# Fetching the second expert layer's first three weight tiles during the last batch's attention

## The chip, the cores and the metric

The kernel runs on one core of one Trainium2 chip. The metric is device time in microseconds (us): the median of three runs. A core has TensorE (PE, matmuls), VectorE (DVE), ScalarE (ACT), GpSimd (POOL) and SyncE (SP, which here only issues transfers). Transfers (DMAs) are issued from the queues of SP, ACT and POOL.

## The reference

Two layers over `x` (4 batches of 512 tokens, 256 wide), with a context of 1601 rows for each batch. Each layer is a cross-attention and then a mixture of eight experts.

```python
x = x + _L0_xattn_ref(ctx_1024, _layernorm(x), ...)      # 8 heads of 128
x = x + _L0_ffn_ref(_layernorm(x), ...)                  # top 2 of 8 experts, with a capacity
x = x + _L1_xattn_ref(ctx_1024, _layernorm(x), ...)      # 8 heads of 32
x = x + _L1_ffn_ref(_layernorm(x), ...)                  # weights of the 2 best of 8 experts

def _L1_ffn_ref(x, W1, b1, W2, b2, Wr, br):
    logits = xf @ Wr + br
    topv, _ = lax.top_k(logits, TOPK)
    masked = jnp.where(logits >= topv[:, TOPK - 1:TOPK], logits, -jnp.inf)
    weights = jax.nn.softmax(masked, axis=-1)
    h = jax.nn.gelu(jnp.einsum('td,edh->eth', xf, W1) + b1[:, None, :], approximate=False)
    expert_out = jnp.einsum('eth,ehd->etd', h, W2) + b2[:, None, :]
    out = jnp.einsum('etd,te->td', expert_out, weights)
```

All numbers are float32. In the last layer the kernel computes an expert only for the tokens that chose it, in tiles of 256 tokens.

## The kernel before

**Four stages.** The first attention (to about 1640 us), the first expert layer (to about 1936), the second attention (to about 2650) and the second expert layer (to the end). The change touches the last two.

**Memory.** Tiles are taken from pools, and pools lie in the on-chip memory one above the other, in the order in which they are opened; a pool that is closed leaves its place to pools opened later. `gat` (eight tiles of 256 columns), `kv1` (keys `kT0`, `kT1` and values `v1` of the second attention, two buffers of each) and `w1p` (`wT`, the attention's three weight matrices, and `cT`, the context turned round, one buffer) are opened before the first expert layer. `kv1` and `w1p` hang on a stack of their own, `kvst`. The second attention opens its own pools above them (`c_one`, `c_two`, `c_six`) and closes them at its end; then `kvst.close()` (L1381) gives up `kv1` and `w1p` too, and the last stage opens `d_one` to `d_spare` from there up. `d_four` has four buffers `w` for an expert's weights: 4104 columns, which are the first layer's matrix (`WB1`, 2048 columns), the second layer's (2048) and the bias (8). `d_spare` has one more.

**The second attention.** 16 units: batch, half of the heads (`o`), half of the tokens (`f`), each of 13 steps, one for each 128 rows of the context. A step computes scores (`ps_w`, L1188), their exponential (ACT, `pT`), its sum over rows (`sum`, on DVE, every third on POOL) and weighs the values (`ps_o`, L1219). `put(step, f)` places other work between: keys and values of the batch after next or so (`keys_values`, in the middle batches), the queries of the next batch, loads of `keyed` and `asked` (SP), the expert outputs of the first expert layer (`collect`, POOL), and `route2`, the last layer's router, for the batch before (from step 10 of a batch, every second step). `route2` normalizes the tokens into `pay`, chooses experts, gives every token a place, writes the corrected `x` to the output (SP, L514) and sends `pay` row by row to its place in two lists in memory, `rows_a` (the first 256 tokens of each expert from batches 0 to 2) and `rows_b` (the others), by indirect DMAs of POOL (L521). Sends to one list wait for each other. Within this stage the order of PE, DVE, ACT and POOL is that of the program (`in_order`). SP's order, and everything in the last stage, is placed by the framework.

At step 4 of the last batch `load_first_weights` (L1279) fetches the first layer's matrix of expert 0, 2048 columns, into the eight tiles of `gat`.

**The second expert layer.** 21 tiles: 8 of `rows_a`, one for each expert (`first_tile`, fetched by SP), then 13 of `rows_b` (`further_tile`, fetched by POOL, indirect, at places that `table` computes). For each tile: the tokens (`rows`, three buffers) are turned by four PE transposes and one DVE copy (`turned`: `tp2`, `xT2`, L1439 and L1440); `told` copies where each token goes (`to`, L1401, five buffers) and its weight (`share`, L1429); `hidden` is the first layer (`ps_h`, L1451, with Gelu on ACT, L1459, that reads the bias from the weights); `results` is the second layer (`ps_y`, L1470), DVE scales it (`y`, L1497) and POOL adds it to the output (L1483). The loop of L1623 runs, for tile i: first layer of i, two steps of the last batch's routing (`rest`), fetch of tile i+2, tokens of tile i+1 turned, second layer of tile i-1. In `first_tile(0)` the second layer's matrix and the bias come as `w2_first` (the profile calls it `w_first`). What is left over after 21 tiles (`beyond`, `ties`) is done only if the counts ask for it; the counts are computed in `table` and read by `values_load` (L1641).

Of the kernel before, what the change touches and what calls it, by code (L numbers as in the profile page):

```python
# [8 lines left out]
F32 = mybir.dt.float32  # L9
I32 = mybir.dt.int32  # L10
# [6 lines left out]
P = 128  # L17
B, S, D = 4, 512, 256
M = 1601
# [30 lines left out]
T = B * S  # L50
# [8 lines left out]
WB2 = WB1 + FC * D  # L59
WIDE = WB2 + FC  # L60


# [5 lines left out]
def xattn_ffn_twice(ctx: ExitStack, tc: tile.TileContext, a: dict, out: bass.AP):  # L68
# [855 lines left out]

# [124 lines left out]
    with ExitStack() as st:  # L1049
# [229 lines left out]
        def load_first_weights():  # L1279


            for i in range(0, WB1, D):
# [97 lines left out]

    kvst.close()  # L1381


    with ExitStack() as st:
        one = st.enter_context(tc.tile_pool(name="d_one", bufs=1))
        two = st.enter_context(tc.tile_pool(name="d_two", bufs=2))
        three = st.enter_context(tc.tile_pool(name="d_three", bufs=3))
        four = st.enter_context(tc.tile_pool(name="d_four", bufs=4))
        five = st.enter_context(tc.tile_pool(name="d_five", bufs=5))
# [6 lines left out]
        def told(rows, share_of):  # L1396
# [6 lines left out]
            return rows, to, share  # L1403

        def columns(t):
            return lambda i, n: t[:, i : i + n]

        def first_tile(e):

            rows = []  # L1410
            for r in range(GR):
                got = three.tile([P, PAY], F32, tag=f"rows{r}", name=f"rows{r}")
                nc.sync.dma_start(got, rows_a[e * G + r * P : e * G + (r + 1) * P, :])
                rows.append(got)
            if e == 0:
                w2 = one.tile([P, WIDE - WB1], F32, name="w2_first")
                nc.sync.dma_start(w2, a["wall"][:P, WB1:])
                w = lambda i, n: (
                    first_weights[i // D][:, i % D : i % D + n]
                    if i < WB1  # L1420
                    else w2[:, i - WB1 : i - WB1 + n]
                )
            else:
                t = four.tile([P, WIDE], F32, tag="w", name="w_e")
                nc.sync.dma_start(t, a["wall"][e * P : (e + 1) * P, :])
# [77 lines left out]
        def table():  # L1503
# [64 lines left out]
            state.update(mine=mine, w_idx=w_idx, x_idx=x_idx, counts=counts_i)  # L1568

        state = {}  # L1570

        def further_tile(i, three=three, four=four):

            rows = []
            for r in range(GR):
# [11 lines left out]
                rows.append(got)  # L1587
            t = four.tile([P, WIDE], F32, tag="w", name="w_e")
            nc.gpsimd.indirect_dma_start(
# [23 lines left out]
        more = [lambda e=e: first_tile(e) for e in range(2, E)]  # L1613
        more += [lambda i=i: further_tile(i) for i in range(SURE)]
        more.append(lambda: further_tile(SURE, spare, spare))

# [24 lines left out]
        n_tiles = nc.values_load(state["counts"][0:1, 0:1], min_val=0, max_val=NG)  # L1641
        ties = nc.values_load(state["counts"][0:1, 1:2], min_val=0, max_val=E * T)

        def beyond(i, fetched=None):
            with tc.If(n_tiles > i):
                w, xT, to, share = ready(*(fetched or further_tile(i)))
                results(w, to, share, hidden(w, xT))
                if i + 1 < NG:
                    beyond(i + 1)

        beyond(SURE, fetched.pop())

        with tc.If(ties > 0):
            for b in range(B):
                for t0 in range(0, NT, GR):
# [19 lines left out]
                    for e in range(E):  # L1677
                        t = spare.tile([P, WIDE], F32, tag="w", name="w_t")
                        nc.sync.dma_start(t, a["wall"][e * P : (e + 1) * P, :])
# [82 lines left out]
```

## Time and profile before

| what | value |
|---|---|
| median of 3 runs | 2993.43 us (2989.96 to 2995.0) |
| the profiled execution | 2993.88 us, its span 2992.2 us |
| PE busy | 2778.0 us (93%) |
| DVE, ACT, POOL busy | 1456.4, 933.3, 400.0 us |
| first attention, 0 to 1650 | PE 1569.9 us busy |
| first expert layer, 1650 to 1936 | PE 278.8 of 286 |
| second attention, 1936 to 2651 | PE 617.8 of 715, DMA share 0.12 |
| start of the second expert layer, 2651 to 2729 | PE 62.5 of 78, DMA share 0.54 |
| its rest, 2729 to 2992 | PE 249.1 of 263, DMA share 0.52 |
| fetch of one expert's weights by SP (`w_e`) | 2052 KB, 7 times |

Times in the views are microseconds from the start of the span. A line of a timeline gives start, duration, engine, line of the kernel, operation, output and input with their sizes, how often, and in brackets how long the engine had been idle and what ended it. A buffer's number is left out of its name, so `w_g` is the weights in `gat`, and `ps_h` all buffers of that name. The DMA share is the mean busy share of the 16 DMA engines.

### The profile page before, as it was taken

Reading aid. Unit: us, or ns where it says so; the run is one execution under the profiler, and the core shown is the slowest. Engines: PE = TensorE matmul, PEld = TensorE weight load, DVE = VectorE, ACT = ScalarE, POOL = GpSimd, SP = SyncE. Lnnn points to the kernel's source line nnn. Section 1 sums busy time; section 2 is a strip of 40 time slices with the busy share of each in tenths; the row PEclk is TensorE's granted clock in tenths of the full one; section 3 lists DMA queues with packets and bytes.
Section 4 is the critical chain, followed back from the end, with each engine's and each line's share of the span. In section 5 each row is a group of like instructions: output and inputs, shape, how many; then the busy total and the mean of one; then the engine's idle time right before and its main releaser. Section 6 shows DMA issues by size and latency. Waiting matters only on the chain.

```text
span 2992.2 us, 35534 instructions
## 1 busy us (share of the span) xinstructions
PE 2778.0 (93%) x13426; PEld 1839.3 (61%) x13426; DVE 1456.4 (49%) x2324; ACT 933.3 (31%) x1312; POOL 400.0 (13%) x308
## 2 busy tenths in 40 slices
PE   5699999999999999999997999879989898898998
PEld 2466676667766667666665566634444444466887
DVE  4256447544475444554454200178777768741110
ACT  2133234323343233333331221124434344341221
POOL 1000000100001000000000100022314223333442
PEclk9899999999999999999998899979999999898999
DMA  8743334433344333333334333110101110055552
GB/s 297 236 124 95 98 92 103 117 92 89 95 113 109 90 94 91 99 93 97 95 94 120 117 106 115 47 46 17 28 24 41 29 37 23 11 181 169 185 173 72
DMA packets 165103, 295.95 MB, mean 99 GB/s; under 512 B 43287, under 2 KB 81752, under 8 KB 161848
## 3 DMA queue, kind: packets, MB, share of 16 engines
q1 hardware_dynamic: 124024, 204.45, 24.4%
q0 software_dynamic: 16320, 53.42, 5.9%
q10 hardware_dynamic: 24576, 35.68, 4.6%
q8 instruction: 109, 1.79, 0.3%
q14 instruction: 74, 0.61, 0.1%
HBM read 97.86 MB, written 49.76 MB: 49 GB/s over the span
## 4 chain that ended last, share of the span: by engine, by line
PE 82%; DVE 7%; issue 3%; DMA 3%; ACT 3%; SPq 2%; POOL 1%; POOLq 0%; DVEq 0%; ACTq 0%
PE ps_o L772 15%; PE ps_s L735 15%; PE ps_v L718 7%; PE ps_k L685 7%; PE ps_w L1188 6%; PE ps_y L1470 4%; PE ps_h L1451 4%; PE ps_h L970 4%; PE ps_y L983 4%; DVE tops L1149 2%; PE ps_o L1219 2%; DVE sum L1210 2%; PE ps_p L783 2%; PE ps_v L945 2%; PE ps_q L670 2%
## 5 line engine op out<-in xcount | busy, mean ns | idle before, releaser
L743 DVE TENSOR_REDUCE top<-ps_s 128x1 f32<-128x2113 f32 x128 | 301.8, 2358 | 574.8 <-PE ps_s L735 574.8
L772 PE MATMUL ps_o<-pT,v 128*128 128x256 f32 x2176 | 521.5, 382 | 7.7 <-DVE pT L764 7.7
L735 PE MATMUL ps_s<-kT,qT 128*128 128x512 f32 (+1 forms) x1280 | 488.9, 527 | 26.3 <-ACT attn L749 26.0
L772 PEld LDWEIGHTS ps_o<-pT,v 128*128 128x128 f32 x2176 | 411.4, 191 | 124.8 <-issue 70.3
L735 PEld LDWEIGHTS ps_s<-kT,qT 128*128 128x128 f32 x1280 | 241.8, 191 | 275.7 <-issue 239.9
L749 ACT ACTIVATE attn<-ps_s,top 128x2113 f32<-128x2113 f32 x128 | 259.0, 2024 | 486.5 <-DVE top L743 448.8
L764 DVE STREAM_TRANSPOSE pT<-swapped 128x2176 f32<-128x2176 f32 x128 | 312.4, 2441 | 70.8 <-DMA swapped<-attn 60.3
L1149 DVE TENSOR_REDUCE tops<-ps_s 128x2 f32<-128x1024 f32 (+1 forms) x224 | 237.4, 1104 | 135.2 <-PE ps_s L1138 135.0
L685 PE MATMUL ps_k<-kvin,wkv 128*128 128x512 f32 (+1 forms) x640 | 262.0, 534 | 5.0 <-ACT kT L692 5.0
L1188 PE MATMUL ps_w<-asked,keyed 64*128 64x256 f32 (+1 forms) x1664 | 244.2, 415 | 20.5 <-DVE tops L1149 9.5
L718 PE MATMUL ps_v<-wkv,kvin 128*128 128x256 f32 x1088 | 253.5, 381 | 0.0
L1201 ACT ACTIVATE pT<-ps_w 128x1024 f32<-128x1024 f32 (+1 forms) x176 | 179.5, 1024 | 192.5 <-PE ps_w L1188 190.4
L1188 PEld LDWEIGHTS ps_w<-asked,keyed 64*128 64x128 f32 (+1 forms) x1664 | 147.0, 189 | 143.2 <-ACT pT L1201 60.7
L718 PEld LDWEIGHTS ps_v<-wkv,kvin 128*128 128x128 f32 x1088 | 204.9, 190 | 32.7 <-issue 3.3
L1210 DVE TENSOR_TENSOR sum<-sum,pT 128x1024 f32<-128x1024 f32 (+1 forms) x128 | 181.0, 1414 | 10.7 <-ACT pT L1201 3.9
L692 ACT ACTIVATE kT<-ps_k,bqk 128x512 f32<-128x512 f32 (+1 forms) x160 | 97.3, 621 | 268.7 <-DMA swapped<-attn 129.8
L1210 POOL TENSOR_TENSOR sum<-sum,pT 128x1024 f32<-128x1024 f32 x48 | 124.1, 2585 | 345.7 <-ACT pT L1201 345.5
L685 PEld LDWEIGHTS ps_k<-kvin,wkv 128*128 128x128 f32 x640 | 116.5, 192 | 80.9 <-issue 67.1
L1451 PE MATMUL ps_h<-xT,w_e 128*128 128x256 f32 x640 | 143.9, 383 | 10.2 <-issue 10.2
L1138 PE MATMUL ps_s<-kT,qT 32*128 32x512 f32 (+1 forms) x1024 | 140.5, 577 | 12.5 <-ACT kT L936 6.8
L725 ACT COPY v<-ps_v 128x512 f32<-128x512 f32 x144 | 80.0, 561 | 224.9 <-PE ps_v L718 156.2
L1470 PE MATMUL ps_y<-w_e,hT 128*128 128x256 f32 x640 | 144.4, 385 | 0.0
(261 smaller groups left out, 2615.1 us busy)
## 6 DMA issues: line engine op xcount, KB each, us to landing
swapped<-attn SPq DMA_DIRECT2D x1536, 68.0 KB
swapped<-attn ACTq DMA_DIRECT2D x512, 68.0 KB
rows_b<-empty SPq DMA_DIRECT2D x36, 530.0 KB
w<-in_w_dram SPq DMA_DIRECT2D x16, 1024.0 KB
w_e<-in_wall_dram SPq DMA_DIRECT2D x7, 2052.0 KB
cT<-in_ctxT_dram SPq DMA_DIRECT2D x4, 1601.0 KB
keyed<-kT SPq DMA_DIRECT2D x32, 200.1 KB
ctx_b<-in_ctx_dram SPq DMA_DIRECT2D x4, 1536.0 KB
```

The costliest lines, as they stand in the source:

```text
L685: nc.tensor.matmul(ps[:, :n], lhsT=wkv[:, c, hs], rhs=flat_kvin[c][:, j0 : j0 + n], start=c == 0, stop=c == DC - 1,)
L718: nc.tensor.matmul(ps[:, k, :], lhsT=flat_kvin[c][:, j * P : (j + 1) * P], rhs=wkv[:, c, cols], start=c == 0, stop=c == DC - 1,)
L735: nc.tensor.matmul(flat[:, j0 : j0 + n], lhsT=qT[:, t * P : (t + 1) * P], rhs=kT[:, j0 : j0 + n], start=True, stop=True,)
L743: nc.vector.tensor_reduce(top, flat[:, :L], AX.X, ALU.max, negate=True)
L749: nc.scalar.activation(attn[:, :L], flat[:, :L], AF.Exp, bias=top, accum_out=total)
L764: nc.vector.transpose(pT[:, :, k * P : (k + 1) * P].rearrange("p c (a i) -> p a c i", a=4), swapped.rearrange("p a (c i) -> p a c i", i=32),)
L772: nc.tensor.matmul(ps, lhsT=v[:, j - parts[part][0], (h % 2) * DH0 : (h % 2 + 1) * DH0], rhs=pT[:, j, :], start=j == 0, stop=j == NB - 1,)
L1149: nc.vector.tensor_reduce(tops[u][:, t : t + at // n, 2 * pair : 2 * pair + 2, j0 // 512], of, AX.X, ALU.max,)
L1188: nc.tensor.matmul(ps[:r, s, pair * QH : (pair + 1) * QH], lhsT=keyed[o][64 * s : 64 * s + 64, pair, j * P : j * P + r], rhs=asked[u % 3][ ...
L1210: (nc.gpsimd if k else nc.vector).tensor_tensor(to, to, pT[:r], ALU.add)
L1451: nc.tensor.matmul(ps[:, f, :], lhsT=w(at, P), rhs=xT[:, c, :], start=c == 0, stop=c == DC - 1,)
L1470: nc.tensor.matmul(ps, lhsT=hT[:, f, r * P : (r + 1) * P], rhs=w(WB1 + f * D, D), start=f == 0, stop=f == FC - 1,)
```

## The change

Keys and values of a batch become one tile `kv` (6530 columns, two buffers), context and the attention's weights one tile `cw` (4738 columns). `load_first_weights`, still at step 4 of the last batch, now fetches three tiles' weights whole: expert 0's rest and expert 1's into the next buffer of `kv` (that of batch 2), expert 2's into `cw`. `kvst.close()` is gone, and so are `d_four`, `w2_first` and the spare tile's own weights: `room(k)` gives the weights of tile k two buffers of `kv`, `cw`, or the one buffer of the new pool `d_new`, in turn. The fetches of tiles 3 to 7 are kept behind SP's transfer before them in the program (`keep_in_program_order`: an order in the queue, no wait for its end). The integer copy of the counts is made in iteration 18 of the loop and not in `table`.

```diff
+KV = DC * M + NM * D
...
-    wT = w1p.tile([P, 3, DC, D], F32, name="wT")
+    cw = w1p.tile([P, DC * (M + 3 * D)], F32, name="cw")
+    cT = cw[:, : DC * M].rearrange("p (c m) -> p c m", c=DC)
+    wT = cw[:, DC * M :].rearrange("p (k c o) -> p k c o", k=3, c=DC)
...
-        cT = w1p.tile([P, DC, M], F32, tag="cT", name="cT")
         nc.sync.dma_start(cT, a["ctxT"][b].rearrange("(c p) m -> p c m", p=P))
-        kT = [kv1.tile([P, M], F32, tag=f"kT{o}", name=f"kT{o}") for o in range(DC)]
-        v = kv1.tile([P, NM, D], F32, tag="v1", name="v1")
+        kv = kv1.tile([P, KV], F32, tag="kv", name="kv")
+        kT = [kv[:, o * M : (o + 1) * M] for o in range(DC)]
+        v = kv[:, DC * M :].rearrange("p (j d) -> p j d", d=D)
...
             for i in range(0, WB1, D):
                 g = gat.tile([P, D], F32, tag="g", name="w_g")
                 nc.sync.dma_start(g, a["wall"][:P, i : i + D])
-                first_weights.append(g)
+                gs.append(g)
+            t = kv1.tile([P, KV], F32, tag="kv", name="w_kv")
+            rest = t[:, WIDE:]
+            nc.sync.dma_start(rest[:, : WIDE - WB1], a["wall"][:P, WB1:])
+            nc.sync.dma_start(t[:, :WIDE], a["wall"][P : 2 * P, :])
+            nc.sync.dma_start(cw[:, :WIDE], a["wall"][2 * P : 3 * P, :])
...
-    kvst.close()
...
-        four = st.enter_context(tc.tile_pool(name="d_four", bufs=4))
+        new = st.enter_context(tc.tile_pool(name="d_new", bufs=1))
...
+        def room(k):
+            if k % 4 == 2:
+                return cw[:, :WIDE]
+            if k % 4 == 3:
+                return new.tile([P, WIDE], F32, tag="w", name="w_e")
+            return kv1.tile([P, KV], F32, tag="kv", name="w_e")[:, :WIDE]
...
-            if e == 0:
-                w2 = one.tile([P, WIDE - WB1], F32, name="w2_first")
-                nc.sync.dma_start(w2, a["wall"][:P, WB1:])
...
+            if e < len(first_weights):
+                w = first_weights[e]
             else:
-                t = four.tile([P, WIDE], F32, tag="w", name="w_e")
-                nc.sync.dma_start(t, a["wall"][e * P : (e + 1) * P, :])
+                t = room(e)
+                tc.keep_in_program_order(
+                    nc.sync.dma_start(t, a["wall"][e * P : (e + 1) * P, :])
+                )
...
-            counts_i = one.tile([P, 2], I32, name="counts_i")
-            nc.vector.tensor_copy(counts_i, counts)
...
-        more.append(lambda: further_tile(SURE, spare, spare))
+        more.append(lambda: further_tile(SURE, E + SURE, spare))
...
+            if i == E + SURE - 3:
+                counts_i = one.tile([P, 2], I32, name="counts_i")
+                tc.keep_in_program_order(nc.vector.tensor_copy(counts_i, state["counts"]))
```

More of the change, by code (lines that the diff above doesn't have):

```diff
@@ L60 @@
 WIDE = WB2 + FC
+KV = DC * M + NM * D
+assert KV >= 2 * WIDE - WB1
 def rows_of(i, n, tail):
@@ L1279, in load_first_weights @@
         def load_first_weights():
+            gs = []
             for i in range(0, WB1, D):
@@ L1284, in load_first_weights, with first @@
                 nc.sync.dma_start(g, a["wall"][:P, i : i + D])
-                first_weights.append(g)
+                gs.append(g)
[4 more added lines that the diff above has]
+            nc.sync.dma_start(cw[:, :WIDE], a["wall"][2 * P : 3 * P, :])
+            def first(i, n):
+                return gs[i // D][:, i % D : i % D + n] if i < WB1 else rest[:, i - WB1 : i - WB1 + n]
+            first_weights.append(first)
+            first_weights.append(lambda i, n: t[:, i : i + n])
+            first_weights.append(lambda i, n: cw[:, i : i + n])
         def put(step, *fs):
@@ L1414, in first_tile @@
                 rows.append(got)
[L1415 to L1425 removed]
+            if e < len(first_weights):
+                w = first_weights[e]
+            else:
+                t = room(e)
+                tc.keep_in_program_order(
+                    nc.sync.dma_start(t, a["wall"][e * P : (e + 1) * P, :])
+                )
                 w = columns(t)
@@ L1567, in table, with further_tile @@
                 nc.vector.tensor_copy(x_idx[:, r, :], x_at)
-            state.update(mine=mine, w_idx=w_idx, x_idx=x_idx, counts=counts_i)
+            state.update(mine=mine, w_idx=w_idx, x_idx=x_idx, counts=counts)
         state = {}
-        def further_tile(i, three=three, four=four):
+        def further_tile(i, k, three=three):
             rows = []
@@ L1587, in further_tile @@
                 rows.append(got)
-            t = four.tile([P, WIDE], F32, tag="w", name="w_e")
+            t = room(k)
             nc.gpsimd.indirect_dma_start(
@@ L1613, in xattn_ffn_twice @@
         more = [lambda e=e: first_tile(e) for e in range(2, E)]
-        more += [lambda i=i: further_tile(i) for i in range(SURE)]
-        more.append(lambda: further_tile(SURE, spare, spare))
+        more += [lambda i=i: further_tile(i, E + i) for i in range(SURE)]
+        more.append(lambda: further_tile(SURE, E + SURE, spare))
         def ready(w, rows, share_of):
@@ L1636, in xattn_ffn_twice @@
             last = (w, to, share, hT, T - S if i < E else T)
+            if i == E + SURE - 3:
+                counts_i = one.tile([P, 2], I32, name="counts_i")
+                tc.keep_in_program_order(nc.vector.tensor_copy(counts_i, state["counts"]))
         results(*last)
         assert next(rest, None) is None
-        n_tiles = nc.values_load(state["counts"][0:1, 0:1], min_val=0, max_val=NG)
-        ties = nc.values_load(state["counts"][0:1, 1:2], min_val=0, max_val=E * T)
+        n_tiles = nc.values_load(counts_i[0:1, 0:1], min_val=0, max_val=NG)
+        ties = nc.values_load(counts_i[0:1, 1:2], min_val=0, max_val=E * T)
         def beyond(i, fetched=None):
             with tc.If(n_tiles > i):
-                w, xT, to, share = ready(*(fetched or further_tile(i)))
+                w, xT, to, share = ready(*(fetched or further_tile(i, 2 + i % 2)))
                 results(w, to, share, hidden(w, xT))
@@ L1649, in beyond @@
                     beyond(i + 1)
+        assert (E + SURE) % 4 < 2
         beyond(SURE, fetched.pop())
@@ L1677, in xattn_ffn_twice @@
                     for e in range(E):
-                        t = spare.tile([P, WIDE], F32, tag="w", name="w_t")
+                        t = room(2 + e % 2)
                         nc.sync.dma_start(t, a["wall"][e * P : (e + 1) * P, :])
```

## The prediction

> **What bounds the kernel now.** I read the busy time by stretches first. TensorE (PE) is busy 93% of the span, so only a stretch where it is not can give anything back. The columns are the stretch, its length, then busy time of PE, PE's weight loads, VectorE (DVE), ScalarE (ACT) and GpSimd (POOL), granted clock, DMA share, GB/s.
>
> ```profile
> 2651.00:2729.00 78.00, 62.47 (x287) 52.63 (x288) 24.21 (x129) 17.87 (x38) 17.55 (x15) 0.89 0.54 183
> 2729.00:2992.00 263.00, 249.09 (x1185) 218.70 (x1183) 37.78 (x135) 57.12 (x136) 101.15 (x79) 0.98 0.52 158
> ```
>
> After 2729 the second expert layer runs without gaps, 14.26 us a tile (6.91 first layer, 6.91 second, 0.44 transposes). The change can only matter from the end of attention (2644) to 2729, where tile 4's first layer begins. PE in that stretch:
>
> ```profile
> 2650.91 5.45 PE L1451 MATMUL ps_h<-xT,w_g 128*128 128x256 f32 x24
> 2658.43 1.10 PE L161 MATMUL tp<-ident,pay 128*128 128x128 f32 x6 [2.08 <-DVE pay L392]
> 2659.36 1.89 PE L1451 MATMUL ps_h<-xT,w_g 128*128 128x256 f32 x8
> 2661.09 0.38 PE L161 MATMUL tp<-ident,pay 128*128 128x128 f32 x2
> ...
> 2704.88 8.99 PE L1451 MATMUL ps_h<-xT,w_e 128*128 128x256 f32 x32 [9.52 <-issue]
> ...
> 2719.55 0.61 PE L1510 MATMUL ps_x<-over,ones 128*128 128x16 f32 x2 [3.93 <-DVE xT L1440]
> ```
>
> The gaps are 2.08, 9.52 and 3.93 us. None ends with a weight landing, although three tiles' weights are fetched just here. The two long ones end when DVE turns the tokens (`xT`). DVE says why:
>
> ```profile
> 2656.06 0.15 DVE L1401 CAST to<-rows 128x1 int32<-128x1 f32 x1 [3.15 <-DMA rows_b<-pay,place_b]
> ...
> 2703.85 0.15 DVE L1401 CAST to<-rows 128x1 int32<-128x1 f32 x1 [21.81 <-DMA out_dram<-y,to]
> ...
> 2718.68 0.21 DVE L1401 CAST to<-rows 128x1 int32<-128x1 f32 x2 [12.87 <-DMA out_dram<-y,to]
> ```
>
> `to` has five buffers. The sixth tile's `to` takes tile 0's, so it waits until tile 0's sums have been added to the output. It stands ahead of `xT` of tile 3 in DVE's queue; the seventh's does the same to tile 4. Those additions are issued by POOL:
>
> ```profile
> 2671.48 0.97 POOL L521 DMA_INDIRECT rows_b<-pay,place_b  x1 [17.86 <-PE ps_h L1451]
> 2676.53 0.97 POOL L521 DMA_INDIRECT rows_b<-pay,place_b  x1 [4.09 <-DMA rows_b<-pay,place_b]
> ...
> 2704.26 0.99 POOL L521 DMA_INDIRECT rows_b<-pay,place_b  x1 [7.16 <-DMA rows_b<-pay,place_b]
> 2709.03 0.97 POOL L521 DMA_INDIRECT rows_b<-pay,place_b  x1 [3.78 <-DMA rows_b<-pay,place_b]
> ```
>
> Eight sends of the last batch's rows go one after the other, each waiting for the one before, and the additions to the output sit between and behind them. The chain of waits runs through the same names. So the stretch is bound by this: the router's decision for the last batch (`place_b`, 2670.73), eight sends, four additions (the last issued at 2714.81, landed by 2718.6), `to`, `xT`, and 10.5 us later tile 4 (2729.09).
>
> **The change, part by part.**
>
> *Early fetch.* Three added DMAs on SP's queue (SyncE's), 1028 + 2052 + 2052 KB, some 0.33 us of issue each, and some 13 to 20 us of transfer at the 424 to 259 GB/s of 2655 to 2665. They wait for batch 2's last use of `kv` (a `ps_o` at about 2507) and the last use of `wT` (`ps_q`, 2445 to 2447). Cost nothing: from 2510 to 2550 the DMA share is 0.00 to 0.05. Behind them on SP stand the loads of `asked` for units 14 and 15 (2504 and 2537 now); each is used 13 or more steps of some 2.7 us after its buffer comes free, so 35 us of slack cover even a load that stands behind all 20 us; without that cover a late load would cost up to those 20 us. The merged `kv` tile is freed by the last `ps_o`, which PE has passed before the next keys are evacuated: nothing.
>
> *Removed from the transition:* `w_first` and the first two `w_e`, 5.1 MB. SP now:
>
> ```profile
> 2625.04 2.71 SPq L1413 DMA_DIRECT2D rows<-rows_a  x6
> 2644.13 0.33 SPq L1417 DMA_DIRECT2D w_first<-in_wall_dram  x1
> 2655.33 0.81 SPq L1425 DMA_DIRECT2D w_e<-in_wall_dram  x2
> ```
>
> While `w_first` moved, batch 2's third-last send (2643.45, 1.80 of issue) took until 2649.7; the next two took 2.5 us from issue to landing, and the last landed at 2655.19. With 2.5 minus 0.97, about 1.6, after the issue: 2646.9, then 2 x 2.7, gives 2652.3. **Gain 2.9 us** at that point, call it R.
>
> *What waits for R.* The part of the diff that is easy to pass over is the removed `kvst.close()`. The pools of the last stage lie one above the other. Before, the small ones (`d_one` with `w2_first`, `d_two`, `d_three`: 11.7 + 44.9 + 6.5 = 63 KB a partition by their tile shapes) took the 71 KB that keys, values, context and `wT` left. That is why `rows` could be fetched at 2625 and tile 0 could start at 2650.91, while `w_e` and `to`, placed higher in attention's `c_one`, waited for R (2655.33 and 2656.06). The first `w_e` waits for that send although it would lie beneath `pay`, so I read the release as one for the whole pool. After the change keys, values and `cw` stay, and `d_one`, `d_two`, `d_three` (54.8 KB) all fall into `c_one` (58 KB): `rows`, `xT2`, `hT2` and the router's own tiles now wait for R.
>
> Tile 0 by these rows: R 2652.3; two issues of 0.45 and a landing of 2.9 (the median of all `rows` transfers; 4.0 for the one at 2677.43): 2655.7; four transposes 0.9, `xT` 0.7: first layer from 2657.3 instead of 2650.91. PE has then idled for 5.6 us. After 9.52 us idle the next 32 matmuls took 8.99 instead of 7.07; after 3.93 the next 28 took 9.10 instead of some 6.2. I take 2.4 (1.9 to 2.9).
>
> The router. The four lines of PE above show which goes first when both can run: the last 8 matmuls of tile 0 cut in between 6 and 2 of the router's transposes. So all 32 will now stand in front of them: 2657.3 + 6.9 + 2.4 = 2666.6; eight transposes 1.1, copy 0.7, logits 1.9, and from their end to `place_b` 6.1 as now (2664.6 to 2670.7): 2676.4. **Loss 5.7 us** on the chain that binds, R's gain included.
>
> *The sends.* First to fourth take 16.8 us now (2671.48 to 2688.32), with the fetch of tile 4's weights (2678.14) inside. The send at 2704.26, with a DMA share of 0.11 after it, took 4.8 to the next; one landed in 3.4. In the new order tile 4's fetch stands right behind tile 4's rows, free at about 2668, so it is over before the sends: 3 x 4.5 = 13.5, **gain 3.3** (0 to 6). The fourth to the eighth (20.7) still meet tile 5's weights (2695.43 now, after tile 1's second layer), worth 7.16 against 3.78: unchanged, between a gain of 3.4 and none.
>
> The Trainium skill's DMA: Bandwidth & Descriptors (Queues, rings and completion order) says that a DMA engine switches between queues packet by packet, so a small send would not stand behind a whole 2 MB load. Taken strictly the relief would be near nothing and the sum about 2.4 us worse than mine, some 2999; the 7.16 against 3.78 says that a neighbour does cost something.
>
> *The rest.* Weights of tiles 3 to 20 still have four buffers and are fetched when the second layer of the tile four before ends. Tile 3's, behind its rows on SP at about 2658, needs 8.5 us and is used after 2700. `counts_i`, 0.1 us of DVE, moves to iteration 18; SP, which waited 6.8 us for it, has no transfer left there. The spare tile's weights move to a shared buffer freed 14 us before. All nothing.
>
> *Sum:* +5.7 - 3.3 = +2.4 us. The profiled execution took 2993.88 (span 2992.2); the median is 2993.43, and I set the sum on the median: 2995.9, **2996**. Own range: -6.7 (both reliefs in full: 5.7 - 6 - 3.4 = -3.7, and 3 us less if rows land sooner and the clock holds) to +6.
>
> **The rivals.**
>
> *Faster: the sends stop binding.* If DVE takes `xT` of tiles 3 and 4 ahead of the late `to`, or POOL the additions ahead of the sends, PE alone sets the pace: 2657.3 + 4 x 6.91 + 3 x 6.91 + 1.8 + 6.5 (router and table) + 2.4 = 2716.4 for tile 4, 12.7 less than 2729.09: 2980.7. Half of it is as likely, so about 2984. For it: PE has only 57 us of work in 78. Against: every later tile of the trace has the same order of `to` before `xT`.
>
> *Slower: tile 4's weights fall on the sends.* Now that fetch (2678.14) came after the write of the corrected `x` (2676.95). If SP keeps that order, the write comes 6 us after `place_b`, at 2682.6, and the fetch hits the second to fourth send: no relief of 3.3, and another 2.4 (6.9 against 4.5): 2993.4 + 5.7 + 2.4 = 3001.5. It decides as soon as that write stands in front of tile 4's rows on SP. Against it: those rows are free at about 2668, long before.
>
> *The fetch isn't early.* If the three loads hang on SP until attention ends, the transition keeps its 5.1 MB and still loses tile 0's early start: +5.7 + 2.9 = 3002. Against: nothing but batch 2's values holds them.
>
> **How the numbers follow.** Forecast 0.50, faster rival 0.25, slower rival 0.18, not early 0.07. A measurement here can tell about 0.2%, 6 us, from no change: 2987.4 to 2999.4. The forecast's own range (2987 to 2999.5) lies almost wholly inside; I leave 0.03 of it above. Faster 0.25, same 0.47, slower 0.28. The range takes in half of the faster rival and the slower one: 2982 to 3004.
>
> **What would show it.** `rows` issued just after R at about 2652, not 2625; tile 0's first layer from about 2657 with 32 matmuls in one piece, then the router's transposes; first send of the last batch at about 2677; gaps on PE before tile 3 and at `ps_x` still ended by `xT`, with `to` waiting for the output additions before it; tile 4 at about 2731. Wrong if `rows` still land before 2650, if `place_b` comes before 2671, or if a gap in the attention before 2640 is ended by an `asked` or `keyed` load.

## The result, and the profile after

The changed kernel took 2998.31 us (median of 20 runs, 2994.4 to 3005.27) beside 2996.74 for the kernel before on the same chip (20 runs, 2989.96 to 3003.12): a ratio of 1.0008 with an interval of 1.0001 to 1.0015. Its profiled execution has a span of 2999.8 us at a granted clock of 0.963 (before: 2992.2 at 0.968). That is no difference by the measure of the prediction, and inside its range. But the two traces show that this "nothing" is made of several sizeable parts, and not quite of those forecast.

Busy time by stretches, in the columns explained with the prediction: from the last `ps_o` of the attention (2657.9, before 2644.07) to tile 4, and from there to the end.

```profile
2658.00:2737.00 79.00, 64.25 (x312) 53.88 (x313) 28.68 (x141) 20.30 (x41) 18.99 (x17) 0.87 0.44 139
2737.00:2999.00 262.00, 249.03 (x1186) 218.94 (x1184) 38.04 (x136) 57.10 (x136) 102.03 (x79) 0.98 0.53 158
```

The second stretch is what it was. From the last `ps_o` to tile 4 it took 84.9 us before and takes 79.2 now; the attention ends 13.8 us later. PE in the first stretch (the lines of the helper functions have moved: first layer L1472, second L1491, `xT` L1461, `to` L1416, sends L523, additions to the output L1504):

```profile
2669.34 1.25 PE L1460 MATMUL tp<-ident,rows 128*128 128x128 f32 x4 [4.63 <-DVE mv L123]
2671.57 8.56 PE L1472 MATMUL ps_h<-xT,w_g 128*128 128x256 f32 x32 [0.98 <-DVE xT L1461]
2679.97 1.04 PE L163 MATMUL tp<-ident,pay 128*128 128x128 f32 x8
...
2714.71 7.07 PE L1472 MATMUL ps_h<-xT,w_e 128*128 128x256 f32 x32
...
2729.12 0.61 PE L1531 MATMUL ps_x<-over,ones 128*128 128x16 f32 x2 [5.59 <-DVE xT L1461]
...
2737.11 7.07 PE L1472 MATMUL ps_h<-xT,w_e 128*128 128x256 f32 x32
```

Tile 0 now comes as one piece of 32, 13.7 us behind the attention's end instead of 6.8, and the router's transposes stand behind it. The gap of 9.52 us before tile 3 is gone (2714.71 follows without one); that before `ps_x` is 5.59 where it was 3.93. VectorE shows that the binding chain is still the same, `xT` of tile 4 behind a `to` that waits for the output:

```profile
2710.41 0.21 DVE L1416 CAST to<-rows 128x1 int32<-128x1 f32 x2 [9.01 <-DMA out_dram<-y,to]
...
2728.26 0.21 DVE L1416 CAST to<-rows 128x1 int32<-128x1 f32 x2 [12.61 <-DMA out_dram<-y,to]
```

POOL's sends of the last batch, and the last of the four additions; then SP's weights:

```profile
2690.65 0.97 POOL L523 DMA_INDIRECT rows_b<-pay,place_b  x1 [25.99 <-DMA w_e<-in_wall_dram]
2693.79 0.97 POOL L523 DMA_INDIRECT rows_b<-pay,place_b  x1 [2.17 <-DMA rows_b<-pay,place_b]
2696.58 0.97 POOL L523 DMA_INDIRECT rows_b<-pay,place_b  x1 [1.83 <-DMA rows_b<-pay,place_b]
2700.72 0.97 POOL L523 DMA_INDIRECT rows_b<-pay,place_b  x1 [3.17 <-DMA rows_b<-pay,place_b]
...
2715.07 0.97 POOL L523 DMA_INDIRECT rows_b<-pay,place_b  x1 [2.47 <-DMA rows_b<-pay,place_b]
...
2724.46 1.56 POOL L1504 DMA_INDIRECT out_dram<-y,to  x1 [6.55 <-DMA out_dram<-y,to]
```

```profile
2667.11 4.11 SPq L1437 DMA_DIRECT2D rows<-rows_a  x8
2671.27 0.42 SPq L1445 DMA_DIRECT2D w_e<-in_wall_dram  x1
...
2682.78 0.43 SPq L1445 DMA_DIRECT2D w_e<-in_wall_dram  x1
...
2696.20 0.39 SPq L516 DMA_DIRECT2D out_dram<-x  x1
...
2714.94 0.33 SPq L1445 DMA_DIRECT2D w_e<-in_wall_dram  x1
```

The sends are 2.8 to 4.6 us apart where they were 3.6 to 8.2. Tile 5's weights, issued at 2714.94, no longer meet any send but the last; they meet the additions instead, and the fourth addition waits 6.55 us where it waited 2.94. The account of these two profiles, behind the attention's end: router's decision +5.2, sends -13.1, additions +3.6, cold clock behind the last gap -1.4: -5.7. It is an account of one pair of executions. A second pair, from e5 and e1 below, has the same signs and other sizes: first send +5.8, sends -11.2, additions +3.8, and -1.8 in all.

Two of these lines need care. The first send's row names `w_e` as what released it, but no weights held it: it is issued 0.74 us after `place_b` was done (2689.91), as in e3, whose row names another releaser. And SP's order has changed around the sends. In the changed kernel tile 4's weights are issued before the first send (2682.78) and the write of `x` after it (2696.20). In the kernel before, both are issued behind the first send (2671.48), the write first:

```profile
2676.95 0.39 SPq L514 DMA_DIRECT2D out_dram<-x  x1
...
2678.14 1.12 SPq L1425 DMA_DIRECT2D w_e<-in_wall_dram  x1
```

So two questions stood open. What relieved the sends, and is it the early fetch? And if the stretch is shorter, by 1.8 us in one pair and by 5.7 in the other, why is the time not?

### The profile page after: what moved, and what is told of

It reads as the page before. It is cut to its first block, busy times and chain, and to the rows that moved or that the text cites. A ratio compares the mean times of both kernels' runs of the same rounds, so it can differ in the third digit from the quotient of the medians.

```text
span 2999.8 us, 35550 instructions
## 1 busy us (share of the span) xinstructions
PE 2787.4 (93%) x13426; PEld 1841.4 (61%) x13426; DVE 1458.2 (49%) x2324; ACT 933.5 (31%) x1312; POOL 399.0 (13%) x308
## 3 DMA queue, kind: packets, MB, share of 16 engines
q1 hardware_dynamic: 124024, 204.45, 24.4%
## 5 line engine op out<-in xcount | busy, mean ns | idle before, releaser
L1214 DVE TENSOR_TENSOR sum<-sum,pT 128x1024 f32<-128x1024 f32 (+1 forms) x128 | 183.5, 1434 | 10.7 <-ACT pT L1205 4.0
L1142 PE MATMUL ps_s<-kv,qT 32*128 32x512 f32 (+1 forms) x1024 | 145.7, 597 | 14.1 <-ACT kv L940 6.8
L727 ACT COPY v<-ps_v 128x512 f32<-128x512 f32 x144 | 79.8, 561 | 225.6 <-PE ps_v L720 159.6
L987 PE MATMUL ps_y<-w,hT 128*128 128x256 f32 x512 | 112.8, 379 | 0.0
L974 PE MATMUL ps_h<-sxT,w 128*128 128x512 f32 x256 | 111.8, 594 | 0.5 <-issue 0.4
```

What stands on the lines that cost most here:

```text
L1142: nc.tensor.matmul(pss[i // 2][:, i % 2, at : at + n], lhsT=qTs[b][rows, o, q0 : q0 + P], rhs=kvs[b][0][o][rows, j0 : j0 + n], start=True, ...
L1214: (nc.gpsimd if k else nc.vector).tensor_tensor(to, to, pT[:r], ALU.add)
```

## The experiments

To compare executions whose clock differs, I measure every profile from the last `ps_n` (the norm sum that follows the last `ps_o` of the attention) to the end of the span, called the tail, and note when that `ps_n` began.

| kernel | last ps_n | to tile 4 | tail | ratio to before (95%) |
|---|---|---|---|---|
| before | 2647.10 | 81.8 | 345.1 | |
| before again (e5) | 2651.41 | 79.1 | 342.5 | |
| merged tiles alone (e2) | 2655.15 | 79.8 | 343.2 | 1.0014 (1.0004 to 1.0023) |
| the same again (e11) | 2655.67 | 79.9 | 345.9 | 1.0001 (0.9991 to 1.0011) |
| changed | 2660.99 | 76.1 | 338.8 | 1.0008 (1.0001 to 1.0015) |
| changed again (e1) | 2658.21 | 77.2 | 339.7 | 1.0000 (0.9991 to 1.0009) |
| early fetch three times (e4) | 2657.47 | 77.3 | 340.0 | 1.0003 (0.9993 to 1.0012) |
| fetch after attention (e3) | 2651.69 | 77.6 | 339.9 | 1.0009 (1.0000 to 1.0017) |
| before, ten buffers (e6) | 2654.71 | 60.7 | 332.8 | 0.9972 (0.9961 to 0.9983) |
| before, ten buffers, late `to` (e10) | 2652.31 | 63.0 | 336.4 | 0.9972 (0.9963 to 0.9982) |
| changed, ten buffers (e7) | 2655.44 | 69.4 | 332.0 | 0.9977 (0.9967 to 0.9987) |
| changed, tile 0 early (e8) | 2657.71 | 72.7 | 334.9 | 0.9979 (0.9970 to 0.9988) |
| the same, ten buffers, late `to` (e9) | 2658.09 | 63.5 | 325.9 | 0.9961 (0.9948 to 0.9974) |
| e9 with two of the three loads after attention (e12) | 2649.32 | 63.0 | 328.1 | 0.9962 (0.9950 to 0.9974) |

The tail of the kernel before and of the merged tiles alone is 342.5 to 345.9 (mean 344.2), that of the changed kernel and of e4 338.8 to 340.0 (mean 339.5): 4.7 us shorter in the mean, with every profile of the second kind below every one of the first.

**e1, the changed kernel again.** No edit.

> The changed kernel once more, with a second profile. Theory A (the early fetch or the merged tiles cost the attention what the transition gains): the attention again ends 8 to 14 us later than in the profile of before (2644.07), with the two late steps again at the tenth and twelfth unit, just behind the fetches; ratio 1.000 to 1.002. Rival B (the attention's 13.8 us were the clock's luck in one execution): the attention ends within 5 us of 2644, the two steps are gone or stand elsewhere, and with a transition 5 us shorter this execution is some 5 us faster than the first one, about 2990 to 2994. Both expect from the end of attention to tile 4's first layer 78 to 81 us, where before it was 84.9.

It takes a share of both theories. The step of the attention at the tenth unit came again (41.0 us for that unit, before 38.0), the one at the twelfth did not (52.1 us, 58.4 in the first profile, 53.1 before), so that one was a matter of one execution. Measured as the text has it, from the last `ps_o`, the transition took 80.3 us; the ratio is 1.0000.

**e2 and e11, the merged tiles alone, in the kernel before.**

```diff
-        kT = [kv1.tile([P, M], F32, tag=f"kT{o}", name=f"kT{o}") for o in range(DC)]
-        v = kv1.tile([P, NM, D], F32, tag="v1", name="v1")
+        kv = kv1.tile([P, KV], F32, tag="kv", name="kv")
+        kT = [kv[:, o * M : (o + 1) * M] for o in range(DC)]
+        v = kv[:, DC * M :].rearrange("p (j d) -> p j d", d=D)
...
```

(and `cT` and `wT` as slices of one `cw`.)

> The kernel before with keys, values, context and weights merged into the two wide tiles, and nothing else. Theory A1 (the merged tile's releases cost the attention): it ends 6 to 14 us after 2644, the transition stays at 85, ratio 1.002 to 1.005. Theory A2 (the cost is the transfer during attention) and rival B (luck of the clock): no more than 3 us beyond the spread between two executions; ratio 0.999 to 1.001.

> The merged tiles alone once more. In the first run the ratio was 1.0014 with 1.0004 to 1.0023, though its transition was within 2 us of that of before. If the merged tiles cost the attention 3 to 5 us, it is again 1.001 to 1.002 and the clock falls behind PE gaps at more places than in the two profiles of before; if the first was chance, 0.9995 to 1.0007.

The first run spoke for a cost of 4 us, the second for none (1.0001). The tail is that of before. The step at the tenth unit is there in both, without any early fetch: the fetch is not its cause. What it is, the windows show. First e11, around the 2.8 us in which PE waits for `shift`, with the granted clock third from the end:

```profile
2464.00:2467.00 3.00, 2.88 (x32) 1.11 (x24) 2.93 (x5) 1.77 (x2) 1.85 (x2) 1.00 0.10 36
2467.00:2470.00 3.00, 0.28 (x2) 0.28 (x3) 2.74 (x5) 0.00 (x1) 0.97 (x1) 0.87 0.09 29
2470.00:2473.00 3.00, 3.00 (x16) 1.85 (x19) 0.00 (x0) 1.20 (x3) 0.00 (x0) 0.50 0.00 0
```

Then the same place in e7, which has the merged tiles and the early fetch on top (here the DMA share is 0.92):

```profile
2465.00:2468.00 3.00, 2.88 (x32) 1.11 (x24) 2.93 (x5) 1.77 (x2) 1.86 (x2) 1.00 0.92 378
2468.00:2471.00 3.00, 0.28 (x3) 0.28 (x4) 2.74 (x5) 0.00 (x1) 0.00 (x0) 1.00 0.67 283
2471.00:2474.00 3.00, 2.83 (x22) 1.44 (x22) 0.45 (x1) 2.18 (x3) 1.20 (x2) 1.00 0.09 29
```

The same instructions with the same gap: in one execution the clock falls to 0.50 for some 6 us, in the other it stays at 1.00. It is worth some 3 us (41.0 against 38.0 for that unit), and it stood there in nine of ten profiles with merged tiles, in part in one of four without.

**e5, the kernel before again.** No edit.

> The kernel before once more, for a second profile. In all five profiles with the merged tiles the clock fell to 0.50 behind a PE gap of 2.8 us in the tenth unit, in four of them at 1992 too; in the one profile of before at neither. If the merged tiles do that, this profile shows the clock at 1.00 at both places, and the attention ends within 2 us of 2644. If the first profile of before was a lucky one (2993.88 where its median over 35 runs is 2997.77), the clock falls at one or both, the attention ends 3 to 8 us later, and the transition is again 83 to 86 us from the end of attention to tile 4.

Neither case as written: the clock stayed at 1.00 at both places, but it fell elsewhere (the seventh unit took 40.8 us, 38.0 in the first profile, with the clock at 0.50 from 2284), and the last `ps_n` began 4.3 us later than in the first profile. So the first profile of before was indeed a short one, and a difference of some 4 us in the attention can't be read from two executions.

**e3, the three fetches behind each tile's rows, after the attention.**

```diff
-            nc.sync.dma_start(t[:, :WIDE], a["wall"][P : 2 * P, :])
+            late.append(lambda: nc.sync.dma_start(t[:, :WIDE], a["wall"][P : 2 * P, :]))
...
             if e < len(first_weights):
+                tc.keep_in_program_order(late[e]())
                 w = first_weights[e]
```

> The changed kernel with the three fetches moved behind each tile's rows, after attention. Theory A2 (the transfer during attention costs 5 to 7 us): attention ends as before, at 2644 plus or minus 2; the transition has its 5.1 MB back beside the sends and takes 86 to 91 us, tile 0 waits for its weights until about 8 us after the last send of batch 2; ratio to before 1.0005 to 1.002. Rival B: the attention differs from that of the changed kernel by chance alone, the transition is 7 to 12 us longer, and the ratio is 1.003 to 1.005, that is 1.002 to 1.004 times the changed kernel.

The attention's end is no help between the theories (it varies too much), but the transition is: tail 339.9, as short as with the early fetch. Neither theory had that. SP and POOL say why:

```profile
2658.21 0.43 SPq L1294 DMA_DIRECT2D w_kv<-in_wall_dram  x1
...
2659.63 0.73 SPq L1295 DMA_DIRECT2D w_kv<-in_wall_dram  x1
...
2661.40 0.43 SPq L1296 DMA_DIRECT2D cw<-in_wall_dram  x1
...
2687.23 0.39 SPq L516 DMA_DIRECT2D out_dram<-x  x1
...
2688.22 0.93 SPq L1447 DMA_DIRECT2D w_e<-in_wall_dram  x1
```

```profile
2681.83 0.97 POOL L523 DMA_INDIRECT rows_b<-pay,place_b  x1 [26.54 <-PE ps_h L1474]
...
2687.79 0.97 POOL L523 DMA_INDIRECT rows_b<-pay,place_b  x1 [1.90 <-DMA rows_b<-pay,place_b]
2693.21 0.97 POOL L523 DMA_INDIRECT rows_b<-pay,place_b  x1 [4.45 <-DMA rows_b<-pay,place_b]
...
2708.53 0.97 POOL L523 DMA_INDIRECT rows_b<-pay,place_b  x1 [2.52 <-DMA rows_b<-pay,place_b]
```

Three loads, issued by 2662, with the DMA share at 0.79 or more in every microsecond from 2661 to 2680, 0.46 in the next and 0.02 behind it; the first send of the last batch is issued at 2681.83. The 5.1 MB have landed before the sends begin, and no gap of PE ends with them. So to fetch them 140 to 200 us earlier (2462 and 2516 in the changed kernel) gains nothing that these times can tell. Two things limit the comparison. In e3, too, tile 0 still waits for R, so its sends begin late; in the kernel before they begin 5 to 6 us sooner after the attention, when the same loads are not quite through. And in e3 the write of `x` and tile 4's weights are issued behind the first send again, as in the kernel before: the send at 2687.79 is 5.42 us from the next, where the changed kernel has 4.14.

**e4, the three early fetches issued three times each** (a loop around the three lines).

> The changed kernel with each of the three early fetches issued three times. Theory A2 (transfer during attention costs, some 5 to 7 us for 5.1 MB): 10 to 14 us on top, ratio to before 1.004 to 1.006, with more late steps just behind the fetches. Rival B: the fetches are hidden, nothing but 10 MB more in idle queues; the same ratio as the changed kernel within 0.001, and no later end of attention but by the clock.

Rival B, as written: 1.0003, tail 340.0. Another 10 MB during the attention cost nothing that these runs can tell, so the 5.1 MB don't either.

**e6 and e7, ten buffers for `to` and its share**, in the kernel before and in the changed one.

```diff
+        many = st.enter_context(tc.tile_pool(name="d_many", bufs=10))
...
-            to = five.tile([P, GR], I32, tag="to", name="to")
-            share = five.tile([P, GR], F32, tag="share", name="share")
+            to = many.tile([P, GR], I32, tag="to", name="to")
+            share = many.tile([P, GR], F32, tag="share", name="share")
```

> The kernel before with ten buffers for `to` and its share instead of five, so that no `to` waits for an addition to the output. If the chain of sends, additions, `to` and `xT` binds as the prediction has it, the gaps on PE before tile 3 (9.52) and in tile 2's second layer (3.93) go, with the cold clock behind them, some 13 to 17 us less in the transition: ratio 0.9945 to 0.996. If they are bound by something else that ends at the same time (the write of x, the rows, the weights), ratio 0.998 to 1.0005.

> The changed kernel with ten buffers for `to`. If the chain still binds there, the one gap left (5.59 us before ps_x, with 0.6 of cold clock behind it) goes: 6 us less than the changed kernel, ratio to before 0.998 to 0.999. The pace is then PE's alone, and since tile 0 starts later than in the kernel before, this one is slower than the kernel before with ten buffers by 4 to 8 us. If the gap has another cause, the ratio stays at 1.000 to 1.001.

PE in e6:

```profile
2700.53 7.07 PE L1452 MATMUL ps_h<-xT,w_e 128*128 128x256 f32 x32
...
2709.18 0.29 PE L1511 MATMUL ps_x<-over,ones 128*128 128x16 f32 x2
...
2715.45 7.07 PE L1452 MATMUL ps_h<-xT,w_e 128*128 128x256 f32 x32
...
2745.07 8.66 PE L1471 MATMUL ps_y<-w_e,hT 128*128 128x256 f32 x32 [7.86 <-DVE y L1498]
```

Both gaps are gone, tile 4 begins 60.7 us after the last `ps_n` instead of 79 to 82: the chain over `to` did bind, and it was worth some 20 us there. Half of it is paid back 30 us later, 7.86 us in tile 4's second layer and 1.6 of cold clock behind it (8.66 where a warm one takes 7.07), so that the ratio is 0.9972 and not the 0.9945 to 0.996 I expected: `y` stands on VectorE behind the `to` of tile 8, whose rows POOL gathers only at 2732 to 2737, behind additions and an indirect fetch of weights (2728.06). In the changed kernel (e7) the gap goes too, and no other appears; its ratio, 0.9977, is below the 0.998 to 0.999 expected. Its late tile 0 now shows: 69.4 against 60.7 us to tile 4. Over the whole tail the two are equal (332.0 and 332.8), not 4 to 8 us apart as I had written, since e6 has its new gap.

**e8, the changed kernel with tile 0 freed of its wait for R** (R is, as in the prediction, the landing of batch 2's last send): its rows lie in `cw` beyond the weights, its `xT` and `hT` in columns of the two wide `kv` tiles.

```diff
-                got = three.tile([P, PAY], F32, tag=f"rows{r}", name=f"rows{r}")
+                if e:
+                    got = three.tile([P, PAY], F32, tag=f"rows{r}", name=f"rows{r}")
+                else:
+                    got = cw[:, WIDE + r * PAY : WIDE + (r + 1) * PAY]
...
+            if two is None:
+                hT = k4[:, WIDE : WIDE + FC * G].rearrange("p (f g) -> p f g", f=FC)
...
```

> The changed kernel, but tile 0's rows, turned tokens and hidden layer lie in columns that the early weights leave free in the wide tiles, so that tile 0 does not wait for R. The prediction's loss of 5.7 us on the way to the router's decision is real if this gives it back: `rows` of tile 0 issued before the attention ends, its first layer within 8 us of the last ps_n (12.5 and 13.1 in the profiles of the changed kernel and 10.5 in to10's, 3.8 before), first send about 24 to 26 us after the last ps_n (29.7 in the changed kernel), tile 4 some 5 us earlier, 70 to 73 us after the last ps_n; ratio to before 0.998 to 0.9995. If the late start of tile 0 was hidden behind the sends anyway, tile 4 stays at 76 to 77 and the ratio at 1.000 to 1.001.

The first layer began 3.6 us after the last `ps_n`, the first send 27.1 us after it (29.7 and 30.4 in the changed kernel; 24 to 26 was expected), tile 4 72.7. (The 12.5 and 13.1 us in that text are misread: by the traces tile 0 begins 10.6 and 10.7 us after the last `ps_n` in the two profiles of the changed kernel.) SP and PE of e8:

```profile
2635.62 0.80 SPq L1446 DMA_DIRECT2D cw<-rows_a  x2
```

```profile
2670.29 0.61 PE L163 MATMUL tp<-ident,pay 128*128 128x128 f32 x3 [2.59 <-issue]
...
2722.22 0.61 PE L1550 MATMUL ps_x<-over,ones 128*128 128x16 f32 x2 [5.84 <-DVE xT L1477]
...
2730.38 7.07 PE L1491 MATMUL ps_h<-xT,k 128*128 128x256 f32 x32
```

The rows are fetched before the attention ends, and the router's transposes start inside tile 0's first layer again. The tail is 4.6 us shorter than that of the changed kernel (334.9 against the mean of 339.5), and the ratio is 0.9979, just under the range expected: with this one wait undone, the change is a gain. The gap before `ps_x` stays, as it should.

**e9 and e10, `to` and share taken from a tile's rows only after the sums of the tile before**, with ten buffers, on e8 and on the kernel before.

```diff
-            return (w, turned(rows), *told(rows, share_of)[1:])
+            return w, turned(rows), rows, share_of
...
-            last = (w, to, share, hT, T - S if i < E else T)
+            last = (w, *told(rows, share_of)[1:], hT, T - S if i < E else T)
```

> The same with ten buffers for `to`, and each tile's `to` and share taken from its rows only after the sums of the tile before are issued, so that neither `xT` nor `y` stands behind them on VectorE. If the sends no longer bind anything, PE sets the pace: from the last ps_n to tile 4 61 to 64 us (60.7 in the kernel before with ten buffers), no gap at tile 5 after it; ratio 0.994 to 0.996. If POOL's queue still holds something, a gap of several us appears behind tile 4 and the ratio is 0.996 to 0.998, as with ten buffers alone.

> The kernel before with ten buffers and the same late `to`. With ten buffers alone a new gap of 7.86 us stood in tile 4's second layer, ended by `y`, which stood behind a `to` that waited for gathered rows, with 1.6 of cold clock behind it. If that order was its cause, it goes: ratio 0.994 to 0.9955, the same as the early fetch with the same two edits, so that the early fetch is worth nothing once the sends are off the path. If the gathered rows are late in themselves, the gap moves to `xT` of that tile, and the ratio stays at 0.997.

e9 is the fastest kernel of the study beside e12: 2985.49 us, ratio 0.9961, no idle time of PE that its timeline marks from the router's transposes to tile 6 (63.5 us to tile 4); the ratio lies just outside the 0.994 to 0.996 expected. Most of the step from e8 is what ten buffers give: the tail is 9.0 us shorter than that of e8, and in e7 ten buffers alone took 7.5 off that of the changed kernel. e10 misses: 0.9972, as with the ten buffers alone, with the gap of 7.8 us where it was. The edit did not do what it says: on VectorE the `to` of tile 8 still stands in front of that `y` (2743.67 and 2744.37). It does so in e9 as well (2736.16 and 2737.81), where the rows that it reads are gathered ten us sooner (2722.95, in e10 2732.43). So the late `to` isn't shown to do anything in either kernel, and whether another order would remove the gap was not tried.

**e12, e9 with the fetches of e3.**

> The version of e9 (tile 0 early, ten buffers, late `to`; there 325.9 us from the last ps_n to the end and a ratio of 0.9961 with 0.9948 to 0.9974), but with the three early fetches issued behind each tile's rows again. If weights beside the sends cost the sends nothing that is felt, the end is 326 to 328 us behind the last ps_n and the ratio 0.995 to 0.997: the early fetch is worth nothing of itself. If the fetch does help now that sends and `to` are out of the way, tile 1 or 2 waits for its weights, 330 to 336 us, ratio 0.9975 to 0.999.

The same time as e9 (0.9962 against 0.9961; tail 328.1 against 325.9, of which 2.85 us is a gap in tile 4's second layer: `y` again stands behind a `to` that waits for gathered rows, 2735.74 and 2736.41). The edit does less than its heading says: the first of the three loads, 1 MB for expert 0, still goes at 2628.13, before the attention's end, behind tile 0's rows; the other two go at 2655.92 and 2657.34. The eight sends take 31.9 us here against 23.9 in e9, with tile 4's weights behind the first send as in e3; with ten buffers they no longer bind. Once more the hour of the fetch makes no difference that the times show.

## Why the prediction held, and where it did not

The time came out as forecast, 1.6 us above before (0.0 to 2.4 by the two ratios) for 2.4 predicted. The chain and the new wait were forecast rightly; that the number came out as well is partly luck. The stretch that the sum was about became shorter, by 1.8 to 5.7 us, where it was to be 2.4 longer, and what lies before it, which the sum put at nothing, became longer and made up for it.

- *What binds.* Right, and shown by e6: without the wait for `to`, both gaps and some 20 us go.
- *The early fetch costs nothing.* Right, shown by e4. That it also brings nothing of itself (e3, e12) the prediction did not say; it priced the loads beside the transition at 5.7 + 2.9 in its last rival (3002), while e3 has the same tail as the changed kernel. The row that I should have weighed was the first send (2671.48 before): by then most of the three loads was through, though not all: the DMA share from 2672 to 2674 was still 0.78.
- *R.* The last send of batch 2 is issued at 2663.69 and lands 2.9 us later, 8.7 us after the attention's end, before 11.1: gain 2.4, predicted 2.9.
- *Tile 0 and the router wait for R.* Right in each point: `rows` issued at 2667.11 just behind R, 32 matmuls in one piece, then the eight transposes; `place_b` 31.9 us after the attention's end instead of 26.7. That is 5.2 for the predicted 5.7, and undoing it (e8) gave back 4.6 of the tail. The cold clock took 1.5 (8.56 against 7.07) instead of 2.4, and 2.2 in e1 (9.25).
- *The sends.* This is the term that was mis-sized: 13.1 us of relief in place of 3.3, or 11.2 by the second pair of profiles (24.1 us in e1 against 35.3 in e5). First to fourth took 10.1 us (9.9 in e1) where I had 13.5 from "3 x 4.5": the 4.5 leaned on one slow send (2704.26, 4.77 to the next) that had a DMA share of 0.11 behind it, and the first sends of the changed kernel, with no load beside them, are 2.8 to 3.1 us apart. Fourth to eighth took 14.35 (14.25 in e1) where I left 20.7 (19.9 in e5) unchanged because they "still meet tile 5's weights". Those weights do keep their distance, 24.3 us behind the first send (24.0 before); but with the first sends sooner through, the eighth is out by 24.4 us, and only the additions meet them. That collision, 3.6 us, was not foreseen: I asked what is late next for the stall I added, not for the one I shortened.
- *Which edit relieves them.* This is not shown; what the fourteen profiles show is what it goes with. From first to eighth the sends take 23.6 to 24.9 us in the six with the early fetch, 26.7 in e3 and 31.9 in e12, 33.9 and 34.2 with the merged tiles alone, and 35.3 to 37.6 in the four of the kernel before with its variants. In those six, tile 4's weights are issued 7.9 us before the first send, and the write of `x` comes later; in the other eight they are issued 5.9 to 7.4 us behind the first send and behind that write, and there one or more later sends take 5 to 9 us. That order, which the framework chose, is the nearest cause in the rows, but no run changes it alone. The removed 5.1 MB can have a direct part of some 2 us, by the first to the second send: 5.05 us before and 4.53 in e5, 3.50 and 3.70 with the merged tiles alone, 2.99 and 3.14 in the changed kernel. It is hardly the whole: in e3 the loads are back in the transition, if through before its sends, and the sends take 26.7. What keeps e3 below the merged tiles alone was not taken apart either: it shares with the changed kernel the later place of the last stage's pools, the shared buffers and the pinned order of later weights.
- *The other side.* The tail became 4.7 us shorter, the time did not. So what lies before the last `ps_n` must have become some 5 to 7 us longer in the mean. The profiles agree (mean 2651.4 in four without merged tiles, 2656.0 in ten with them, spread over 8 and 12 us), and where I followed a difference within the attention, it was a lower clock behind PE gaps that are the same in both. Whether the merged tiles bring that about stays open: alone they measured 1.0014 and 1.0001. Most of it arises inside this attention: from its first `ps_w` to the last `ps_n` it takes 666.2 to 669.6 us in the four (mean 667.8) and 668.3 to 677.1 in the ten (mean 671.9), and two falls of the clock, in the first and in the tenth unit, some 3 us each, make most of the difference. The only steady difference that I found is small: the eighth unit takes 30.5 us in all ten and 30.3 in all four.

The faster rival (the sends stop binding) had part of its 12.7 us come true in the stretch, 1.8 to 5.7 us, by faster sends and not by another order on VectorE or POOL. The slower rival's order, the write of `x` in front of tile 4's weights, did not occur in the changed kernel: these were issued at 2682.78, the write at 2696.20. It did occur in e3 and e12, whose edit moves only the fetches. In e3 it goes with sends that take 2.3 us more than in the changed kernel, where the rival had priced it at 3.3 + 2.4.

## What to carry to other kernels

Before a load is moved earlier, look for who waits for it: here no wait of PE in the profile ended with a weight landing, and the early fetch was worth nothing that the times can tell, however well it was hidden. What the change did to the time lay in its side effects, above all in what its space was used for before: a pool that moves on top of another inherits that pool's last reader (5 us here, and a gain of 0.2% once undone). And where a chain of small transfers binds, price one of them from a row in which nothing else moves, and follow which neighbour each of them still meets when the ones before it get faster. Look also where a load stands on its issuing queue: a wait that moves can put it ahead of those small transfers or among them, without any line of the edit saying so.

## What was not expected of the hardware

One send of 132.5 KB, issue to issue, takes 2.8 to 3.1 us with no load beside it (the first two of the changed kernel and of e3) and 5.4 to 8.9 beside a weight load of 2 MB (the third and the sixth in the two profiles of before, the third in e2, e11 and e3). The Trainium skill's DMA: Bandwidth & Descriptors (Queues, rings and completion order) has the engines change between queues packet by packet, so that a send need not stand behind a whole load. The rows agree in part. The third send of before, issued at 2681.43, moved nothing until 2685.5, while 1.36 MB of the load went; after that its 0.14 MB moved beside 0.68 MB of SP's transfers. In e3 the third send was through 4 us before the load was. But the sixth send of before, issued at 2696.08 beside the load of 2695.43, moved its bytes only after 2702.5, when 2.08 MB of that load had gone and 0.02 MB were left: it came almost as late as behind the whole. So a send beside a load took 2.4 to some 6 us longer here than one without, and the two sends that meet one in the profile of before (6.9 and 8.2 us) make some 8 of the 13.1 us of relief (4.1 and 3.2 us for the same two in the changed kernel). What makes a send's first bytes late is not shown.

The granted clock fell behind one gap of 2.8 us in some executions and not in others, with all instructions around it alike (e7 and e11 above); such a fall costs some 3 us, and the runs of the kernel before spread over 13 us. The Trainium skill's TensorE: Matmul & The Clock Gate (What's actually happening) says that the activity window of about 3.4 us runs freely, without regard to the kernel, which would make it a matter of phase; the two windows fit that, but no run here shows the phase itself. That the fall at this place came in nine of ten profiles with merged tiles and in part in one of four without fits a free phase less well; its cause stays open.
